# First attention of a two-layer Flamingo block: softmax weights turned by VectorE blocks and SBUF transfers, with scores two batches ahead of values

## The chip, the core and the metric

The kernel runs on one core of one Trainium2 chip. The metric is the device time of one execution in microseconds. The core has five engines that work side by side, each in its own order: TensorE (PE for the matmul, PEld for the load of the stationary operand), VectorE (DVE), ScalarE (ACT), GpSimd (POOL) and SyncE (SP), which here issues transfers. They wait for one another through semaphores. Matrix products land in PSUM, in tiles of 128 partitions × 512 float32 values[...]. Everything is float32.

## The reference, cut to what matters

The inputs are `x` of 16 batches × 128 tokens × 512 and a latent context `ctx` of 16 × 128 × 128. Two layers follow each other, each an attention and a feed-forward part, each added to `x` through a tanh gate. Only the first attention is changed:

```python
q_hk  = (layernorm(x) @ Wq.T).reshape(b, s, 16, 128)
q_big = einsum('bshk,hkq->bshq', q_hk, w_kc_q)
kv    = rope(ctx)                                   # b, l, 128
q_r   = einsum('bshq,hqr->bhsr', q_big, W_qr)       # r = 64
k_r   = einsum('bld,hdr->bhlr', kv, W_kr)
attn  = softmax(einsum('bhsr,bhlr->bhsl', q_r, k_r))
ctx_c = einsum('bhsl,bld->bhsd', attn, kv)
out   = einsum('bhsd,hkd->bshk', ctx_c, w_kc_kv).reshape(b, s, 2048) @ Wo.T
x     = x + tanh(g) * out
```

After it come a mixture-of-experts part with low-rank updates (f0), a causal attention with 16 heads of 32 (a1) and a feed-forward part of eight low-rank experts (f1).

## The kernel before, in words

**Stages.** The profiled execution has five stages: folding of weights until 97.9 us, first attention until 597.3, f0 until 1334, a1 until 1641, f1 until the end at 1860. The batches stand in four groups (`NG`) of four (`GB`); the 16 heads stand in eight pairs (`NPAIR`).

**Folds.** The three query projections of a head are multiplied into one matrix `fq` while weights load ("inward" fold). As a pair's `fq` is done, the keys (`key`) and queries (`query`) of group 0 for that pair follow. Then the "outward" fold multiplies the value projection of each head into the output projection: for each pair, SP loads `wckv_p` and `wo_p` (four buffers each), TensorE makes `o_ps` (L304), and `evacuate` copies it to `fo`. `evacuate` gives its copies to VectorE (L75) and ScalarE (L77) in turn.

**A group.** For groups 1 to 3 the kernel loads the latents, rotates them on GpSimd (`rope`), transposes them (`kvtr`, L189), normalises and transposes four batches of `x` (`layernorm_T`, `xtr`, L133), and makes eight pairs of `k_ps` (L196) and `q_ps` (L204). This is the long stretch of keys and queries. Then come the four batches. `attend` works on half a batch, that is eight heads: 16 score matmuls (L349) into two PSUM tiles of four heads each, then for each tile `exp_normalised`: the maximum on VectorE (`nmx`, L143), four exponentials on ScalarE (L148), the reciprocal of the sum on VectorE (`rden`, L153), and the multiplication on GpSimd (L155). The result `e` has queries on its partitions.

**Transposes and values.** The product with the latents needs latent positions on the partitions. `gather` therefore transposes each of a tile's four heads on TensorE against the identity (`etr`, L368), copies the tile out (`eT`), multiplies it with the rotated latents (`c_ps`, L372) and copies that out (`c`). After both halves of a batch, sixteen matmuls add the heads up to `y_ps` (L391), and VectorE adds that to `x` (`residual`, L138).

**Order.** The loop makes the scores of the next half batch ahead of `gather` of the present one. Beyond that, a scheduler places instructions by their dependencies, and PSUM buffers decide: four tiles in `ps_mm` (scores, keys, queries, `y_ps`, `o_ps`), two in `ps_tr` (transposes), two in `ps_acc` (`c_ps`).

**Loads for f0.** They stand on SP's queue (L315 to L329) once the outward fold has been issued: `w1` (4 MB), the factors `a1`, `b1`, `a2`, `b2`, and small ones. The load of `w2` waits for the last `y_ps`, since it takes the place of `fo`.

Of the kernel before, what the change touches and what calls it, by code (L numbers as in the profile page):

```python
# [15 lines left out]
P = 128  # L16
NB = 16
# [13 lines left out]
LORA_SCALE = 2.0  # L31
HD = 32
K2 = 8
R2 = 64
EPS = 1e-5
MASKED = -3.4028234663852886e38
# [3 lines left out]
def kernel(  # L40
# [93 lines left out]
            evacuate(xnT[:, :, ts(i, P)], tr.rearrange("p (c t) -> p c t", t=P))  # L134
        return xnT

    def residual(b, ps, gate):
        nc.vector.scalar_tensor_tensor(xt[b], ps, gate, xt[b], ALU.mult, ALU.add)  # L138

# [20 lines left out]
    with tc.tile_pool(name="a0", bufs=2) as ap, tc.tile_pool(name="a0s", bufs=3) as sp:  # L160

        def load_kv(g):
            kv = ap.tile([P, GB, P], F32, tag="kv", name=f"kv_{g}", bufs=1)
            nc.sync.dma_start(
                out=kv, in_=kvc[g * GB : (g + 1) * GB].rearrange("b l d -> l b d")
            )
            return kv

        def rope(g, kv):
            kvr = ap.tile([P, GB, P], F32, tag="kvr", name=f"kvr_{g}", bufs=1)  # L170
            rot = ap.tile([P, GB, P], F32, tag="e", name=f"rot_{g}", bufs=3)
            half = P // 2
            cos_b = cos_sb.unsqueeze(1).to_broadcast([P, GB, P])
            nc.gpsimd.tensor_tensor(kvr, kv, cos_b, ALU.mult)
            for lo, hi in ((0, half), (half, 0)):
                nc.gpsimd.tensor_tensor(
                    rot[:, :, lo : lo + half], kv[:, :, hi : hi + half],
                    sin_sb[:, lo : lo + half].unsqueeze(1).to_broadcast([P, GB, half]),
                    ALU.mult,
                )  # L180
            nc.gpsimd.tensor_tensor(
                kvr[:, :, :half], kvr[:, :, :half], rot[:, :, :half], ALU.subtract
            )
            nc.gpsimd.tensor_tensor(
                kvr[:, :, half:], kvr[:, :, half:], rot[:, :, half:], ALU.add
            )
            tr = tr_tile(f"kvtr_{g}")
            for i in range(GB):
                nc.tensor.transpose(tr[:, ts(i, P)], kvr[:, i, :], ident)  # L189
            kvT = ap.tile([P, GT], F32, tag="kv", name=f"kvT_{g}", bufs=1)  # L190
            evacuate(kvT, tr)
            return kvr, kvT

        def key(g, p, kvT):
            k_ps = mm_tile(f"k_ps{g}_{p}")
            nc.tensor.matmul(k_ps, wkr_sb[:, ts(p, P)], kvT, start=True, stop=True)  # L196
            k_p = ap.tile([P, GT], F32, tag=f"k{p}", name=f"k_{g}_{p}", bufs=1)
            evacuate(k_p, k_ps)
            return k_p

        def query(g, p, xnT):
            q_ps = mm_tile(f"q_ps{g}_{p}")
            for c in range(ND):
                nc.tensor.matmul(  # L204
                    q_ps, fq[:, c, ts(p, P)], xnT[:, c, :],
                    start=(c == 0), stop=(c == ND - 1),
                )
# [5 lines left out]

        kvr_0 = kvT_0 = xnT_0 = None
        k_0, q_0 = [], []
        with tc.tile_pool(name="fold", bufs=3, side="right") as fp:
            kv_0 = load_kv(0)
            for b in range(GB):
# [57 lines left out]
            for p in range(1, 3):  # L276
                load_pair(p)
            m_next = fold_first(0)
            kvr_0, kvT_0 = rope(0, kv_0)
            for p in range(NPAIR):  # L280
                m_now = m_next
                if p + 3 < NPAIR:
# [6 lines left out]
                    xnT_0 = layernorm_T("a0", 0)  # L289
                q_0.append(query(0, p, xnT_0))  # L290

            for p in range(NPAIR):
                wckv_p = fp.tile([P, 2, P], F32, tag="wckv", name=f"wckv_{p}", bufs=4)
                nc.sync.dma_start(
                    out=wckv_p, in_=wckv[2 * p : 2 * p + 2].rearrange("h k d -> k h d")
                )
                wo_p = fp.tile([P, 2, D], F32, tag="wo", name=f"wo_{p}", bufs=4)
                nc.sync.dma_start(
                    out=wo_p,
                    in_=woT[2 * p * P : (2 * p + 2) * P, :].rearrange("(h p) d -> p h d", p=P),  # L300
                )
                for j in range(2):
                    o_ps = mm_tile(f"o_ps{p}_{j}")
                    nc.tensor.matmul(  # L304
                        o_ps, wckv_p[:, j, :], wo_p[:, j, :], start=True, stop=True
                    )
                    evacuate(fo[:, 2 * p + j, :], o_ps)

        for b in range(GB, NB):
            nc.scalar.dma_start(out=xt[b], in_=x[b])  # L310


        wf = ctx.enter_context(tc.tile_pool(name="wf", bufs=1, side="right"))
        w1_sb = wf.tile([P, ND, FF], F32, tag="w1_sb", name="w1_sb")
        nc.sync.dma_start(out=w1_sb, in_=f_w1.rearrange("(c p) f -> p c f", p=P))  # L315
        a1_sb = wf.tile([P, ND, E * ER], F32, name="a1_sb")
        nc.sync.dma_start(out=a1_sb, in_=f_a1T.rearrange("(c p) r -> p c r", p=P))
        b1_sb = wf.tile([P, FF], F32, name="b1_sb")
        nc.sync.dma_start(out=b1_sb, in_=f_b1T)
        a2_sb = wf.tile([P, NF, E * ER], F32, name="a2_sb")  # L320
        nc.sync.dma_start(out=a2_sb, in_=f_a2T.rearrange("(c p) r -> p c r", p=P))
        b2_sb = wf.tile([P, D], F32, name="b2_sb")
        nc.sync.dma_start(out=b2_sb, in_=f_b2T)
        nc.sync.dma_start(out=wr_sb, in_=f_wr.rearrange("(c p) e -> p c e", p=P))
        nc.sync.dma_start(out=br_sb, in_=f_br.partition_broadcast(P))
        nc.sync.dma_start(out=bias1_sb, in_=f_b1.rearrange("(c p) -> p c", p=P))
        nc.sync.dma_start(out=bias2_sb, in_=f_b2.partition_broadcast(P))
        nc.sync.dma_start(out=mw2_sb, in_=m_w2.rearrange("(c p) e -> p c e", p=P))
        nc.sync.dma_start(out=mb1_sb, in_=m_b1.rearrange("(c p) -> p c", p=P))  # L329
        nc.sync.dma_start(out=mb2_sb, in_=m_b2.partition_broadcast(P))  # L330

        for g in range(NG):
            if g == 0:
                kvr, k_r, q_r = kvr_0, k_0, q_0
            else:
                kvr, kvT = rope(g, load_kv(g))
                xnT = layernorm_T("a0", g)
                k_r, q_r = [], []
                for p in range(NPAIR):
                    k_r.append(key(g, p, kvT))  # L340
                    q_r.append(query(g, p, xnT))

            def attend(i, hf):
                scores = [mm_tile(f"s_ps{g}_{i}_{hf}_{j}") for j in range(2)]
                for n in range(4):
                    p = 4 * hf + n
                    for j in range(2):
                        rows = slice(j * R, (j + 1) * R)
                        nc.tensor.matmul(  # L349
                            scores[j][:, ts(n, P)],  # L350
                            q_r[p][rows, ts(i, P)], k_r[p][rows, ts(i, P)],
                            start=True, stop=True,
                        )
                es = []
                for j in range(2):
                    n = f"{g}_{i}_{hf}_{j}"
                    e = ap.tile([P, 4 * P], F32, tag="e", name=f"e_{n}", bufs=3)
                    exp_normalised(sp, scores[j], e, f"a0_{n}")
                    es.append(e)
                return es  # L360

            def gather(i, hf, es):
                cx = []
                for j in range(2):
                    n = f"{g}_{i}_{hf}_{j}"
                    tr = tr_tile(f"etr_{n}")
                    for m in range(4):
                        nc.tensor.transpose(tr[:, ts(m, P)], es[j][:, ts(m, P)], ident)  # L368
                    eT = ap.tile([P, 4 * P], F32, tag="eT", name=f"eT_{n}")
                    evacuate(eT, tr)  # L370
                    c_ps = acc_tile(f"c_ps{n}")
                    nc.tensor.matmul(c_ps, kvr[:, i, :], eT, start=True, stop=True)  # L372
                    c_sb = ap.tile(
                        [P, 4 * P], F32, tag=f"c{hf}{j}", name=f"c_{n}", bufs=1
                    )
                    evacuate(c_sb, c_ps)
                    cx.append(c_sb)
                return cx

            steps = [(i, hf) for i in range(GB) for hf in range(2)]  # L380
            ahead, cx = attend(*steps[0]), {}
            for s, (i, hf) in enumerate(steps):
                now = ahead
                if s + 1 < len(steps):
                    ahead = attend(*steps[s + 1])
                cx[hf] = gather(i, hf, now)
                if hf == 0:
                    continue
                o_ps = mm_tile(f"y_ps{g}_{i}")
                for h in range(H):  # L390
                    nc.tensor.matmul(  # L391
                        o_ps, cx[h // 8][h % 2][:, ts(h % 8 // 2, P)], fo[:, h, :],
                        start=(h == 0), stop=(h == H - 1),
                    )
                residual(g * GB + i, o_ps, gate_x[0])

    w2_sb = wp.tile([P, NF, D], F32, tag="w32a", name="w2_sb")
    for s in range(2):
# [401 lines left out]
```

## Time and profile before

| what | value |
|---|---|
| median of 3 runs | 1858.1 us (1855.93 to 1862.87) |
| profiled execution, its own time | 1862.03 us |
| its span | 1860.2 us |
| TensorE busy in the span | 1792.7 us, 96% |
| first attention, 97.9 to 597.3 us | 499.4 us |
| its batches (four stretches) | 102.2 + 98.3 + 103.5 + 93.1 us |
| its keys and queries (three stretches) | 34.3 + 33.7 + 34.3 us |

A row of the profile names the line, the engine, the operation, the output and the inputs, the shapes and the count, then the busy time in us and the mean time of one in ns, then the engine's idle time just before these instructions with what ended it. The mean of a matmul is that of one instruction from its start to its modelled end. Matmuls overlap, so what a sequence of them takes is read from the chain of waits or from the timeline, where a run of equal instructions has a start and a length. "x28" counts passes: a float32 matmul with 512 columns is recorded as two.

### The profile page before, as it was taken

The numbers are of one execution on the slowest core, as the hardware profiler recorded it, in microseconds if no ns is written. First come the engines' busy times: TensorE is split into PE (matmuls) and PEld (weight loads), VectorE is DVE, ScalarE is ACT, GpSimd is POOL, SyncE is SP. The second block draws the span as 40 slices with busy tenths as digits, with TensorE's granted clock in tenths as the row PEclk, the third lists the DMA queues.
The fourth block names the chain that finished last, engine by engine and source line by source line (L and its number), as shares of the span: only waits on it lengthen the run. The fifth ranks groups of instructions, "written<-read, shape, count | busy, mean of one in ns | idle before, by whom it ended". The sixth has DMA issues, their size and how long they took to land.

```text
span 1860.2 us, 16590 instructions
## 1 busy us (share of the span) xinstructions
PE 1792.7 (96%) x6240; PEld 905.7 (49%) x6240; DVE 631.2 (34%) x1228; ACT 504.2 (27%) x1526; POOL 245.6 (13%) x249
## 2 busy tenths in 40 slices
PE   6999999999999999999999999999899999999998
PEld 5554454444445444444444444444465655654444
DVE  4232222322322442143224322442254555622221
ACT  2242142232332321032103210321053644611100
POOL 1022022022011111011101110111020311300000
PEclk9999999999999999999999999999979789799999
DMA  9340000000101100000000000001000000000000
GB/s 324 95 156 1 5 3 0 6 1 1 57 1 40 51 1 0 0 0 1 0 0 1 0 0 0 1 0 68 11 1 6 7 1 1 1 0 23 23 23 23
DMA packets 31328, 43.45 MB, mean 23 GB/s; under 512 B 5776, under 2 KB 16784, under 8 KB 30608
## 3 DMA queue, kind: packets, MB, share of 16 engines
q1 hardware_dynamic: 28224, 37.54, 5.9%
q10 hardware_dynamic: 3024, 4.85, 0.7%
q8 instruction: 49, 0.80, 0.2%
q14 instruction: 31, 0.25, 0.0%
HBM read 38.20 MB, written 4.19 MB: 23 GB/s over the span
## 4 chain that ended last, share of the span: by engine, by line
PE 91%; DVE 3%; DMA 2%; ACT 2%; POOL 1%; issue 1%; ACTq 0%; SPq 0%; DVEq 0%; POOLq 0%
PE fy_ps L552 12%; PE y_ps L391 12%; PE h_ps L506 12%; PE t_ps L532 6%; PE l_ps L517 6%; PE q_ps L204 6%; PE vx_ps L707 3%; PE my_ps L724 3%; PE y_ps L656 3%; PE c_ps L372 3%; PE h_ps L675 3%; PE q_ps L597 3%; PE s_ps L615 2%; PE e1tr L639 2%; PE o_ps L647 2%; PE k_ps L196 1%
## 5 line engine op out<-in xcount | busy, mean ns | idle before, releaser
L506 PE MATMUL h_ps<-xnT_f,w_sb 128*128 128x512 f32 x512 | 240.6, 592 | 0.0
L391 PE MATMUL y_ps<-fo,c 128*128 128x512 f32 x512 | 227.0, 594 | 1.6 <-DVE c L75 1.6
L155 POOL TENSOR_TENSOR e<-e,rden_a 128x512 f32<-128x512 f32 x128 | 132.7, 1039 | 714.1 <-DVE rden_a L153 581.6
L552 PE MATMUL fy_ps<-w_sb,mix 128*128 128x512 f32 x512 | 223.0, 592 | 0.0
L521 DVE TENSOR_TENSOR a<-l_ps,base 128x512 f32<-128x512 f32 x128 | 88.5, 692 | 248.7 <-PE l_ps L517 248.3
L552 PEld LDWEIGHTS fy_ps<-w_sb,mix 128*128 128x128 f32 x512 | 97.3, 190 | 122.4 <-issue 121.5
L506 PEld LDWEIGHTS h_ps<-xnT_f,w_sb 128*128 128x128 f32 x512 | 97.0, 190 | 120.5 <-issue 120.5
L391 PEld LDWEIGHTS y_ps<-fo,c 128*128 128x128 f32 x512 | 95.4, 190 | 114.7 <-issue 111.0
L526 POOL TENSOR_TENSOR mix<-a,a 128x512 f32<-128x512 f32 x64 | 80.9, 1264 | 366.6 <-DVE a L523 366.6
L517 PE MATMUL l_ps<-t,b_sb 128*128 128x512 f32 x256 | 121.4, 594 | 0.2 <-DVE t L495 0.2
L532 PE MATMUL t_ps<-a,a_sb 128*128 128x512 f32 x256 | 120.5, 593 | 0.1
L204 PE MATMUL q_ps<-xnT_a,fq 128*128 128x512 f32 x256 | 115.5, 594 | 3.3 <-ACT xnT_a L77 2.0
L148 ACT ACTIVATE e<-s_ps,nmx_a 128x128 f32<-128x128 f32 x256 | 90.2, 394 | 89.8 <-DVE nmx_a L143 82.3
L511 ACT ACTIVATE base<-h_ps,bias_sb 128x512 f32<-128x512 f32 x64 | 44.0, 687 | 225.3 <-PE h_ps L506 225.3
L148 ACT ACTIVATE e<-e,nmx_a 128x128 f32<-128x128 f32 x256 | 98.9, 390 | 13.2 <-DVE nmx_a L143 13.2
L522 ACT ACTIVATE a<-a 128x512 f32<-128x512 f32 x128 | 80.6, 630 | 73.6 <-DVE a L521 73.5
L138 DVE SCALAR_TENSOR_TENSOR x<-y_ps,gates,x 128x512 f32<-128x512 f32 x32 | 24.0, 750 | 225.1 <-PE y_ps L391 191.6
L523 DVE TENSOR_TENSOR a<-a,wT 128x512 f32<-128x512 f32 x128 | 87.8, 686 | 6.3
L560 DVE SCALAR_TENSOR_TENSOR fy<-bias_sb,wsum,fy_ps 128x512 f32<-128x512 f32 x16 | 12.0, 747 | 205.4 <-PE fy_ps L556 205.4
L204 PEld LDWEIGHTS q_ps<-xnT_a,fq 128*128 128x128 f32 x256 | 48.4, 190 | 63.8 <-issue 57.7
L517 PEld LDWEIGHTS l_ps<-t,b_sb 128*128 128x128 f32 x256 | 48.0, 190 | 58.8 <-issue 57.4
L532 PEld LDWEIGHTS t_ps<-a,a_sb 128*128 128x128 f32 x256 | 42.9, 188 | 67.5 <-DVE a L523 63.6
(153 smaller groups left out, 2125.9 us busy)
## 6 DMA issues: line engine op xcount, KB each, us to landing
x<-in_x ACTq DMA_DIRECT2D x16, 256.0 KB, 6.1
wq<-in_wq SPq DMA_DIRECT2D x8, 512.0 KB, 5.7
wo<-in_woT SPq DMA_DIRECT2D x8, 512.0 KB, 5.9
w_sb<-in_f_w SPq DMA_DIRECT2D x1, 4096.0 KB, 12.6
w_sb<-in_f_w SPq DMA_DIRECT2D x2, 2048.0 KB, 12.1
out<-x SPq DMA_DIRECT2D x16, 256.0 KB, 2.0
wcq<-in_wcqT SPq DMA_DIRECT2D x8, 384.0 KB, 6.2
kv<-in_kvc SPq DMA_DIRECT2D x8, 256.0 KB, 2.8
```

The lines of the kernel that those rows point to most:

```text
L148: nc.scalar.activation(dst[:, ts(i, P)], src[:, ts(i, P)], AF.Exp, bias=nmx[:, i : i + 1], accum_out=den[:, i : i + 1],)
L155: nc.gpsimd.tensor_tensor(d3, d3, rden.unsqueeze(2).to_broadcast([P, 4, P]), ALU.mult)
L204: nc.tensor.matmul(q_ps, fq[:, c, ts(p, P)], xnT[:, c, :], start=(c == 0), stop=(c == ND - 1),)
L391: nc.tensor.matmul(o_ps, cx[h // 8][h % 2][:, ts(h % 8 // 2, P)], fo[:, h, :], start=(h == 0), stop=(h == H - 1),)
L506: nc.tensor.matmul(h_ps, w1_sb[:, c, ts(f, P)], xnT[:, c, :], start=(c == 0), stop=(c == ND - 1),)
L517: nc.tensor.matmul(l_ps, b1_sb[:, ts(f, P)], t1[k], start=True, stop=True)
L521: nc.vector.tensor_tensor(a, l_ps, base, ALU.add)
L522: nc.scalar.activation(a, a, AF.Gelu_apprx_tanh)
L523: nc.vector.tensor_tensor(a, a, wT[k], ALU.mult)
L526: nc.gpsimd.tensor_tensor(m, act[0], act[1], ALU.add)
L532: nc.tensor.matmul(t2_ps[k], a2_sb[:, f, :], act[k], start=(f == 0), stop=(f == NF - 1),)
L552: nc.tensor.matmul(y_ps, mix[f][:, ts(i, P)], w2_sb[:, f, :], start=(f == 0), stop=False,)
```

## The change

It does the following in the first attention.

1. The `etr` transposes on TensorE and the `eT` copies go. VectorE transposes each tile of `e` in blocks of 32 × 32 in place (`nc.vector.transpose`, into `eb`), and 16 transfers a batch on SP's queue carry the blocks to their partitions: block row `q`, block column `k` of all 16 heads at once, from `eb` to `eT` (`carry`).
2. Scores are made by whole batches, into all four `ps_mm` tiles, and two batches ahead (`AHEAD`): step `s` does `gather(s - 2)`, `score(s)`, `project(s - 2)`, `carry(s)`. The transposes of the next group's latents and normalised rows stand between `score` and `project` in steps 2 and 3 of a group, the keys and queries after `project` in step 3.
3. The scores of batches 0 and 1 stand ahead of the outward fold. Its first four loads are issued ahead of the small f0 loads, the others as the folds go, and `carry(0)` after the last of them.
4. TensorE's instructions and SP's transfers of this stage keep the order in which they are written (`keep_in_program_order`).
5. `k_ps`, `q_ps`, `c_ps` and `o_ps` move to the two `ps_tr` tiles; `y_ps`, `kvtr` and `xtr` share the two `ps_acc` tiles. `kvr` gets two buffers, and `kvT` one of its own.
6. The loads of `a1`, `w1` (now in quarters), `b1`, `a2` and `b2` are issued in the last step, after `gather(15)` and ahead of `project(15)`.

```diff
+BK = 32
+NK = P // BK
+AHEAD = 2
...
+    def matmul(*args, **kw):
+        ins = nc.tensor.matmul(*args, **kw)
+        if ordered[0]:
+            tc.keep_in_program_order(ins)
...
+    def send(dst, src):
+        ins = nc.sync.dma_start(out=dst, in_=src)
+        if ordered[0]:
+            tc.keep_in_program_order(ins)
...
+        def score(b):
+            g, i = divmod(b, GB)
+            scores = [mm_tile(f"s_ps{b}_{t}") for t in range(4)]
...
+            eb = rp.tile([P, H, P], F32, tag="eb", name=f"eb_{b}")
+            eTs[b] = rp.tile([P, H, P], F32, tag="eT", name=f"eT_{b}")
+            for t in range(4):
+                e = ap.tile([P, 4 * P], F32, tag="e", name=f"e_{b}_{t}", bufs=3)
+                exp_normalised(sp, scores[t], e, f"a0_{b}_{t}")
+                nc.vector.transpose(
+                    eb[:, 4 * t : 4 * t + 4, :], e.rearrange("p (n l) -> p n l", l=P)
+                )
...
+        def carry(b):
+            for q in range(NK):
+                for k in range(NK):
+                    send(eTs[b][ts(k, BK), :, ts(q, BK)], ebs[b][ts(q, BK), :, ts(k, BK)])
+
+        def gather(b):
+            g, i = divmod(b, GB)
+            cxs[b] = []
+            for t in range(4):
+                c_ps = tr_tile(f"c_ps{b}_{t}")
+                matmul(
+                    c_ps, roped[g][0][:, i, :],
+                    eTs[b][:, 4 * t : 4 * t + 4, :].rearrange("p n q -> p (n q)"),
+                    start=True, stop=True,
+                )
+                c_sb = ap.tile([P, 4 * P], F32, tag=f"c{t}", name=f"c_{b}_{t}", bufs=1)
+                evacuate(c_sb, c_ps)
+                cxs[b].append(c_sb)
...
+        ordered[0] = True
+        for s in range(AHEAD):
+            score(s)
+        for p in range(NPAIR):
+            fold_outward(p, *outward[p])
+            if p + 4 < NPAIR:
+                outward.append(load_outward(p + 4))
+            if p == 3:
+                carry(0)
+        for s in range(NB + AHEAD):
+            b = s - AHEAD
+            g = s // GB + 1
+            if b >= 0:
+                gather(b)
+            if AHEAD <= s < NB:
+                score(s)
+            if s == NB + AHEAD - 1:
...
+                send(a1_sb, f_a1T.rearrange("(c p) r -> p c r", p=P))
...
+            if g < NG and s % GB == 2:
+                latents(g)
+            if g < NG and s % GB >= 2:
+                for i in range(2):
+                    normalise(g, s % GB * 2 - 4 + i)
+            if b >= 0:
+                project(b)
+            if 0 < s < NB:
+                carry(s)
+            if g < NG:
+                if s % GB == 0:
+                    kv_next = load_kv(g)
+                elif s % GB == 1:
+                    roped[g] = rope(g, kv_next)
+                    deviations(g)
+                elif s % GB == 3:
+                    k_r[g], q_r[g] = [], []
+                    keys_and_queries(g, range(NPAIR))
+        ordered[0] = False
-            def gather(i, hf, es):
-                cx = []
-                for j in range(2):
-                    n = f"{g}_{i}_{hf}_{j}"
-                    tr = tr_tile(f"etr_{n}")
-                    for m in range(4):
-                        nc.tensor.transpose(tr[:, ts(m, P)], es[j][:, ts(m, P)], ident)
-                    eT = ap.tile([P, 4 * P], F32, tag="eT", name=f"eT_{n}")
-                    evacuate(eT, tr)
...
```

## The prediction

> **What bounds the kernel now.** The page comes first, for the engine that limits:
>
> ```profile
> PE 1792.7 (96%) x6240; PEld 905.7 (49%) x6240; DVE 631.2 (34%) x1228; ACT 504.2 (27%) x1526; POOL 245.6 (13%) x249
> ```
>
> TensorE is busy 96% of the span; VectorE has two thirds of its time free, ScalarE nearly three quarters. The change touches the first attention alone, 97.9 to 597.3 us, so I next cut that stage at its own seams (the key and query stretches of groups 1 to 3 are the second, fourth and sixth piece) and take each engine's busy time from the table of windows:
>
> ```profile
> 97.90:200.10 102.20, 96.49 (x375) 49.74 (x374) 30.34 (x59) 33.76 (x149) 20.69 (x21) 0.97 0.18 67
> 200.10:234.40 34.30, 34.30 (x88) 15.36 (x90) 8.43 (x18) 6.16 (x10) 0.00 (x0) 1.00 0.03 8
> 234.40:332.70 98.30, 93.52 (x369) 48.17 (x367) 29.58 (x62) 35.85 (x150) 20.70 (x21) 0.98 0.00 1
> 366.40:469.90 103.50, 96.53 (x375) 49.84 (x374) 30.29 (x59) 33.96 (x149) 20.69 (x21) 0.97 0.00 1
> 504.20:597.30 93.10, 90.13 (x348) 46.11 (x347) 24.62 (x51) 32.91 (x146) 16.63 (x16) 0.98 0.07 23
> 97.90:597.30 499.40, 478.96 (x1711) 239.36 (x1711) 138.94 (x278) 153.31 (x618) 78.71 (x79) 0.98 0.06 21
> ```
>
> The columns are length, then busy time of PE, PEld, DVE, ACT and POOL, granted clock, DMA share, GB/s. TensorE idles 20.4 us of 499.4, all of it in the four stretches of batches; the DMA engines are all but empty (share 0.06). So time leaves this stage only if TensorE is given less to do or idles less. What it does, by shape:
>
> ```profile
> L391 PE MATMUL y_ps<-fo,c 128*128 128x512 f32 x512 | 227.0, 594 | 1.6 <-DVE c L75 1.6
> L368 PE MATMUL etr<-ident,e 128*128 128x128 f32 x256 | 40.6, 294 | 5.1 <-POOL e L155 4.7
> L75 DVE COPY eT<-etr 128x512 f32<-128x512 f32 x32 | 20.9, 682 | 10.4 <-PE etr L368 10.4
> L77 ACT COPY eT<-etr 128x512 f32<-128x512 f32 x32 | 19.1, 633 | 98.7 <-PE etr L368 98.7
> ```
>
> The transposes of the weights are the only TensorE work that the change removes; their copies out cost engines that have room. Last, the order at the stage's start:
>
> ```profile
> 97.84 2.06 PE L349 MATMUL s_ps<-k,q 64*128 64x128 f32 x32
> 101.31 1.16 PE L349 MATMUL s_ps<-k,q 64*128 64x128 f32 x8 [1.42 <-ACT e L148]
> ...
> 105.97 3.78 PE L372 MATMUL c_ps<-eT,kvr 128*128 128x512 f32 x4
> ```
>
> **The change part by part.** A batch now costs, by chained rows: y_ps 12.02 us for 28 passes, 0.429 each, so 32 make 13.74; c_ps eight passes, 3.43; scores 32 in 2.0 (the 2.06 above).
>
> *Transposes removed.* Eight take 1.04 to 1.34 us in sequence (not their 294 ns each: they overlap), so 16 take 2.3 to 2.6 us, 256 some 37 to 41 by either reckoning, and part of the 5.1 us idle before them goes too. The 64 copies that leave (VectorE 20.9, ScalarE 19.1 us) free time that nobody waits for.
>
> *VectorE's transposes added.* Four a batch, 128x512; no row shows the operation. Below: the 539 ns of a normalisation between SBUF tiles; above: twice the 682 ns copy. I take the copy. Four make 2.8 us a batch in place of 1.4 us of copies, on an engine with some 70% free: nothing on the path, 0 to +3 us a batch of delay to the transfers.
>
> *Transfers added.* 256 on SP's queue, 16 a batch, each 512 pieces of 128 bytes (64 KB): 512 pieces for each of 16 DMA engines a batch. They wait for the batch's fourth transpose, and c_ps two steps later waits for the last of them. Issue is 16 × 0.47, some 7.5 us a batch. For the pieces, the nearest row is a latent load, 512 pieces of 512 bytes, alone on the queues:
>
> ```profile
> 1336.00:1336.50 0.50, 0.00 (x0) 0.00 (x0) 0.00 (x0) 0.00 (x0) 0.00 (x0) 0.50 0.11 31
> 1336.50:1337.00 0.50, 0.00 (x0) 0.00 (x0) 0.00 (x0) 0.00 (x0) 0.00 (x0) 0.50 0.36 108
> 1337.00:1337.50 0.50, 0.00 (x0) 0.00 (x0) 0.00 (x0) 0.00 (x0) 0.00 (x0) 0.50 1.01 304
> 1337.50:1338.00 0.50, 0.00 (x0) 0.00 (x0) 0.00 (x0) 0.00 (x0) 0.00 (x0) 0.50 0.28 82
> ```
>
> Shares 0.11 + 0.36 + 1.01 + 0.28 of 0.5 us on 16 engines are 14.1 engine-us, 27.5 ns a piece. At the same 27.5 ns for 128 bytes a batch occupies the queues 14.1 us[...]. From above, a bias load of 2048 four-byte pieces held SP's next issue 3.50 us, 128 pieces an engine, at most 27 ns each. I take 14 us and keep 7 to 30. The window is wide: from the end of a batch's scores, weights are ready after about 7.5 us and read after two steps less the scores, 33 us, so 26 us; and in the long run a batch may take a step, 19.7 us (38 ns a piece). By this the transfers are hidden.
>
> [...] The row speaks for overlap: 256 KB moved in about 2 us with issue at 0.4 us spacing[...]. I go by the row[...].
>
> *Scores two batches ahead, order kept.* Gather waits vanish if transfers are in time, but TensorE, now strictly in order, picks up others: where the next group's latents and normalised rows are transposed (three times), the two-buffer PSUM pool waits for a copy on ScalarE queued behind all four tiles' exponentials. Scores' first tile is ready at 0.5 us, maximum 0.69, sixteen exponentials at 0.344 make 5.5, copy 0.59: 7.3 us after the scores began, against 2.0 of scores and about 1 of transposes, a wait of 4.3; 4.9 in the middle group, where VectorE's queue adds 0.6. The following step waits about 0.9 for a normalised copy. Sum 13.5 + 2.7 = 16 us. TensorE pauses then bring the second price:
>
> ```profile
> 104.00:110.00 6.00, 5.92 (x15) 3.11 (x15) 1.92 (x5) 3.91 (x19) 2.08 (x2) 0.50 0.99 413
> ```
>
> After a 1.4 us pause the granted clock is 0.50 for some 6.4 us (c_ps above took 3.78 us instead of 1.7): 3.3 us lost. [...] I take 10.5. (Before lost about 10 in the same way.)
>
> *Outward folds behind the first scores.* Scores of batch 0 start near 82.5 instead of 97.8; those of batch 1 wait for tiles to be read, to about 91. The 16 folds are 13.7 us of passes, but their evacuations queue behind exponentials and transposes, and pairs 4 to 7 load only as buffers come free; end about 112. SP queues batch 0's transfers behind the last pair's issue; they leave from about 105 to 115 and land near 118, so gather(0) starts at 118 where it started at 106. That costs 12 us, against two batches of scores already done (4.0) and folds that no longer follow.
>
> *Moved loads.* The MoE weights are asked for after gather(15) instead of at 98 us. SP holds nothing else then; y_ps(15) covers 13.7 us, and w1's first quarter (1 MB, about 3 us at the 413 GB/s above) is needed some 13 us after the stage's end: nothing, at worst +10. The next latents' loads and rotation start a step or more before their use: nothing.
>
> **Sum.** From 118: sixteen steps of 3.43 + 2.0 + 13.74 + 0.5 of small waits = 19.7, 315.2, less 4.0 of scores done, 311.2; three key and query stretches at 34.3, 102.9; 60 transposes for them at 0.145, 8.7; waits 16; clock 10.5. The stage ends at 567.3, against 597.3: 30 us less on the profiled span of 1860.2 (own time 1862.0, within the runs shown: 1855.9 to 1862.9). From the median of 1858.1: **1828 us**.
>
> **The rivals.**
> *Cheaper pauses.* If the copies interleave better or a pause brings no half clock, 10 to 18 us of the last two terms stay away: about 1814. For it: VectorE shares the evacuations. Against: the order on each engine is fixed.
> *Transfers somewhat late.* At 24 us a batch they fit the mean (a group has 79 + 37 us for 96) but not four steps in a row: two steps a group late by about 2.4 and 4.3 us, 27 us over four groups, of which 10 fall into waits already counted: about 1845.
> *Transfers as the bound (slower).* The place is c_ps waiting for SP's queue. With X us a batch the stage ends near 122 + 16X, even with before at X = 29.7: 58 ns a piece, 1.86 us a transfer. At 64 ns X is 32.8, the end 647, the time 1908; at 75 ns some 1991. For it: no run shows 128-byte pieces between SBUF tiles, each piece from 32 partitions only[...]. Against: 27 ns at most in both rows.
> That TensorE is not relieved cannot be: 256 of its instructions are gone.
>
> **How the numbers follow.** Forecast 0.58, cheaper pauses 0.16, somewhat late 0.13, transfers as the bound 0.13. A difference under 0.5%, 9.3 us, cannot be told from none in this kernel. Faster takes the first two and half of the third: 0.80; same the other half and a little: 0.07; slower 0.13. The range, 1805 to 1866, takes in the first three with the unknown prices (start ±8, waits −16 to +10, moved loads to +10) and leaves out the fourth and a tail below.
>
> **What would show it.** Right: no etr row, c_ps without long waits for DMA, stage end near 567, batch steps near 20 us, three clock dips of some 6 us a group apart. Wrong: SP's transfers 1.5 us or more apart and c_ps idle behind them; score matmuls waiting on exponentials in every step; h_ps waiting for w1; gather(0) far from 118.

## Result and the profile after

The changed kernel takes 1836.5 us, median of four runs (1834.9 to 1839.3), beside 1860.5 for the kernel before (1855.9 to 1863.0): a ratio of 0.9875, 95% interval 0.9849 to 0.9901, or 24 us less. Forecast were 30 us less and 1828, with 1805 to 1866 as the range. The profiled execution has a span of 1833.1 us, 27.1 below that of before; the other 3 us are the place of the two profiled executions among their runs.

The rows by shape of the changed kernel, from 80 to 620 us; the columns are those of before:

```profile
L144 PE MATMUL y_ps<-fo,c 128*128 128x512 f32 x512 | 230.8, 610 | 5.4 <-DVE xnT_a L78 3.2 <-ACT kvT L80 2.1
L144 PE MATMUL c_ps<-eT,kvr 128*128 128x512 f32 x128 | 63.7, 634 | 8.2 <-DMA eT<-eb 7.3 <-DVE c L78 0.9
L401 DVE STREAM_TRANSPOSE eb<-e 128x512 f32<-128x512 f32 x64 | 45.5, 710 | 58.5 <-POOL e L176 57.4 <-DMA eT<-eb 1.1
L144 PEld LDWEIGHTS q_ps<-xnT_a,fq 128*128 128x128 f32 x192 | 34.7, 189 | 50.2 <-issue 35.9 <-ACT q L80 9.0 <-DVE q L78 5.3
L149 PE MATMUL xtr_a<-ident,xn_a 128*128 128x128 f32 x48 | 8.0, 304 | 9.5 <-DVE xnT_a L78 6.3 <-DVE kvT L78 3.2
```

The `etr` row is gone. In its place VectorE has 64 block transposes of 0.71 us, close to the copy that the forecast took. Of all values only the first waited for a transfer (7.3 us). What the other steps wait for stands at `xtr_a` and `y_ps`: copies on VectorE and ScalarE. The page's list of transfers adds their time to landing:

```profile
eT<-eb SPq DMA_DIRECT2D x256, 64.0 KB, 2.3
```

The windows of the stage, cut at its own seams (length, busy PE, PEld, DVE, ACT, POOL, granted clock, DMA share, GB/s):

```profile
80.40:118.50 38.10, 25.12 (x97) 11.90 (x96) 17.22 (x33) 16.32 (x72) 8.31 (x8) 0.81 0.46 98
118.50:171.40 52.90, 47.74 (x165) 23.37 (x166) 20.86 (x43) 18.05 (x74) 12.45 (x13) 0.88 0.34 51
171.40:206.30 34.90, 34.90 (x81) 14.60 (x80) 6.88 (x10) 4.10 (x7) 0.00 (x0) 1.00 0.13 20
206.30:294.50 88.20, 83.11 (x308) 39.94 (x308) 37.14 (x74) 31.90 (x142) 20.72 (x21) 0.96 0.28 43
294.50:330.40 35.90, 35.90 (x82) 14.81 (x81) 6.29 (x9) 4.69 (x8) 0.00 (x0) 1.00 0.14 20
330.40:420.00 89.60, 84.03 (x309) 40.10 (x308) 37.17 (x74) 31.80 (x142) 20.73 (x21) 0.96 0.28 43
420.00:455.00 35.00, 35.00 (x82) 14.69 (x81) 6.88 (x10) 4.10 (x7) 0.00 (x0) 1.00 0.18 35
455.00:567.90 112.90, 112.90 (x370) 52.01 (x369) 34.78 (x66) 30.43 (x141) 16.62 (x16) 1.00 0.43 99
```

The stage ends at 567.9 us (forecast 567.3). The last window is the change as it was meant: TensorE is busy throughout at full clock, although transfers fill 43% of the DMA engines' time (the loads for f0 at its end among them). What is left of pauses and half clock in this stage lies in the rows with a clock below 1.00: the start, and the end of each of the first three groups. TensorE's timeline there:

```profile
118.55 6.53 PE L144 MATMUL c_ps<-eT,kvr 128*128 128x512 f32 x8 [7.27 <-DMA eT<-eb]
125.01 2.06 PE L144 MATMUL s_ps<-k,q 64*128 64x128 f32 x32
127.00 0.66 PE L149 MATMUL kvtr<-ident,kvr 128*128 128x128 f32 x4
127.49 0.60 PE L149 MATMUL xtr_a<-ident,xn_a 128*128 128x128 f32 x4
131.26 1.11 PE L149 MATMUL xtr_a<-ident,xn_a 128*128 128x128 f32 x4 [3.17 <-DVE xnT_a L78]
133.22 16.34 PE L144 MATMUL y_ps<-fo,c 128*128 128x512 f32 x32 [0.84 <-ACT kvT L80]
```

Two waits of 3.17 and 0.84 us stand between scores and outputs. The copies that end them:

```profile
129.86 0.71 DVE L401 STREAM_TRANSPOSE eb<-e 128x512 f32<-128x512 f32 x1 [0.56 <-POOL e L176]
130.55 0.66 DVE L78 COPY xnT_a<-xtr_a 128x512 f32<-128x512 f32 x1
132.49 0.68 ACT L80 COPY kvT<-kvtr 128x512 f32<-128x512 f32 x1
```

The long wait ends with VectorE's copy, which stands behind the block transpose of the new batch's first tile, and that behind GpSimd's multiplication. The short one ends with ScalarE's copy, behind the exponentials of all four tiles. The outputs then take 16.34 us where this view has 14.00 in an undisturbed step. The granted clock in one-microsecond windows says why:

```profile
136.00:137.00 1.00, 1.00 (x3) 0.48 (x2) 0.94 (x3) 0.00 (x0) 0.03 (x1) 0.50 0.00 0
137.00:138.00 1.00, 1.00 (x3) 0.47 (x2) 0.60 (x3) 0.30 (x1) 0.00 (x0) 0.52 0.00 0
138.00:139.00 1.00, 1.00 (x3) 0.38 (x2) 0.17 (x1) 0.00 (x0) 0.00 (x0) 1.00 0.75 107
```

From 132 to 138 us it is one half (the last column but two).

### The profile page after: what moved, and what is told of

Read it like the earlier page. It is cut to its first block, busy times and chain, and to the rows that moved or that the text cites. A ratio compares the mean times of both kernels' runs of the same rounds, so it can differ in the third digit from the quotient of the medians.

```text
span 1833.1 us, 16301 instructions
## 1 busy us (share of the span) xinstructions
PE 1758.6 (96%) x5984; PEld 870.6 (47%) x5984; DVE 653.8 (36%) x1260; ACT 488.6 (27%) x1494; POOL 245.7 (13%) x249
## 4 chain that ended last, share of the span: by engine, by line
PE 88%; DVE 4%; DMA 2%; SPq 2%; ACT 2%; POOL 1%; issue 1%; ACTq 0%; POOLq 0%; DVEq 0%
PE fy_ps L652 12%; PE h_ps L606 12%; PE y_ps L144 11%; PE q_ps L144 6%; PE t_ps L632 6%; PE l_ps L617 6%; PE vx_ps L807 3%; PE my_ps L824 3%; PE y_ps L756 3%; PE h_ps L775 3%; PE q_ps L697 3%; PE c_ps L144 3%; PE s_ps L715 2%; PE e1tr L739 2%; SPq L154 2%; PE o_ps L747 2%
## 5 line engine op out<-in xcount | busy, mean ns | idle before, releaser
L144 PE MATMUL y_ps<-fo,c 128*128 128x512 f32 x512 | 230.8, 610 | 5.4 <-DVE xnT_a L78 3.2
L176 POOL TENSOR_TENSOR e<-e,rden_a 128x512 f32<-128x512 f32 x128 | 133.2, 1043 | 696.6 <-DVE rden_a L174 648.0
L144 PE MATMUL q_ps<-xnT_a,fq 128*128 128x512 f32 x256 | 118.5, 606 | 3.5 <-DVE mv_a L354 3.5
## 6 DMA issues: line engine op xcount, KB each, us to landing
w_sb<-in_f_w SPq DMA_DIRECT2D x4, 1024.0 KB, 10.7
```

Of the source, the lines that this page charges most:

```text
L144: ins = nc.tensor.matmul(*args, **kw)
L176: nc.gpsimd.tensor_tensor(d3, d3, rden.unsqueeze(2).to_broadcast([P, 4, P]), ALU.mult)
```

## Experiments

The theory: the gain is TensorE's transposes, which now lie beside its other work because two steps of lookahead cover the transfers; part of it is paid back at the start and at three waits with their half clock. The rivals: the lookahead and the fixed order gain by themselves; or the transfers are near the point where they set the pace. All times are medians; the changed kernel's is 1836.5, and before was 1860.1 to 1861.1 beside each of these.

### Transposes back on TensorE, in the new order

```diff
-                e = ap.tile([P, 4 * P], F32, tag="e", name=f"e_{b}_{t}", bufs=3)
+                e = eb[:, 4 * t : 4 * t + 4, :].rearrange("p n l -> p (n l)")
                 exp_normalised(sp, scores[t], e, f"a0_{b}_{t}")
-                nc.vector.transpose(
-                    eb[:, 4 * t : 4 * t + 4, :], e.rearrange("p (n l) -> p n l", l=P)
-                )
...
-                    send(eTs[b][ts(k, BK), :, ts(q, BK)], ebs[b][ts(q, BK), :, ts(k, BK)])
+            for t in range(4):
+                tr = tr_tile(f"etr_{b}_{t}")
+                for m in range(4):
+                    transpose(tr[:, ts(m, P)], ebs[b][:, 4 * t + m, :], ident)
+                evacuate(
+                    eTs[b][:, 4 * t : 4 * t + 4, :],
+                    tr.rearrange("p (n q) -> p n q", q=P),
+                )
```

> The changed kernel's order and lookahead, with the weights transposed on TensorE again, in the place where the transfers were issued. Theory (the gain is the TensorE work that went to VectorE and the queues): 16 x (2.3 to 2.6) = 37 to 42 us come back, less some 7 us since the first values no longer wait for transfers; 1865 to 1880 us, slower than the kernel before. Rival (the gain is the lookahead of two batches and the fixed order): at most 1850.

Measured: 1867.3 us, a ratio to before of 1.0040 (1.0024 to 1.0055). The rival falls: order, lookahead and the moved folds by themselves make the kernel some 7 us slower, and moving the transposes off TensorE is worth 31. Its TensorE timeline shows the work that came back:

```profile
249.40 1.04 PE L149 MATMUL etr<-ident,eb 128*128 128x128 f32 x8
251.09 1.06 PE L149 MATMUL etr<-ident,eb 128*128 128x128 f32 x8 [0.66 <-DVE eT L78]
252.50 3.89 PE L144 MATMUL c_ps<-eT,kvr 128*128 128x512 f32 x8 [0.34 <-DVE eT L78]
```

From one batch's values to the next this step takes 22.75 us (229.75 to 252.50), where the changed kernel's takes 19.54: 2.1 us of transposes and 1.0 of waits for their copies.

### One step of lookahead

```diff
-AHEAD = 2
+AHEAD = 1
```

> AHEAD = 1 in place of 2. Theory (the transfers are hidden by the second batch of lookahead): in the changed kernel a batch's last transfer lands 24.4 us after its scores begin (229.4 to 253.8); with one step between, values are due after 15.9, so TensorE waits 8.5 us in some 12 steps, about 100 us, and each such wait brings 2 to 3 us of half clock: 1935 to 1970. Rival (the transfers are short enough for one step): within 20 us of 1836.

Measured: 1928.9 us, 92 more than the changed kernel; a little less than expected, and far from the rival. Its waits:

```profile
PE c_ps L144 <- DMA eT<-eb: 86.4, 12, 9.9
```

Twelve waits for transfers, 7.2 us each. So the transfers are not short; the second batch of lookahead hides them.

### Transposes for the next group ahead of the scores

```diff
+            if g < NG and s % GB == 2:
+                latents(g)
+                normalise(g, 0)
+            if g < NG and s % GB == 3:
+                normalise(g, 2)
+                normalise(g, 3)
             if AHEAD <= s < NB:
                 score(s)
...
             if g < NG and s % GB == 2:
-                latents(g)
-            if g < NG and s % GB >= 2:
-                for i in range(2):
-                    normalise(g, s % GB * 2 - 4 + i)
+                normalise(g, 1)
```

> The transposes of the next group's latents and rows put ahead of the scores of steps 2 and 3 (the second row's behind), so that their copies stand ahead of the exponentials. Theory: the waits there (12.4 us in the three steps 2, 3.3 in the three steps 3) and the half clock behind them (2.6 + 2.1 + 3.1) go, 23 us: 1812 to 1820. Rival (the pause only moves, to the PSUM tile or to the values' copies): 1830 to 1840.

Measured: 1808.8 us, a ratio of 0.9728 (0.9709 to 0.9747): 27.7 us less than the changed kernel, more than was expected. The same place in its timeline has no wait, and the outputs follow at once at full clock:

```profile
125.19 0.60 PE L149 MATMUL kvtr<-ident,kvr 128*128 128x128 f32 x4
125.62 0.60 PE L149 MATMUL xtr_a<-ident,xn_a 128*128 128x128 f32 x4
126.15 2.06 PE L144 MATMUL s_ps<-k,q 64*128 64x128 f32 x32
128.14 0.66 PE L149 MATMUL xtr_a<-ident,xn_a 128*128 128x128 f32 x4
128.63 13.90 PE L144 MATMUL y_ps<-fo,c 128*128 128x512 f32 x32
```

So the waits were a matter of order on ScalarE and VectorE: a copy behind the new scores' exponentials and block transposes is late, the same copy ahead of them is not. The stage ends 24.9 us earlier (its last outputs end at 543.0). Of the remaining 2.8 us, 1.9 lie behind the stage (1263.3 us to the end of the span instead of 1265.2) and 0.9 between the runs.

### The first transfers ahead of the late outward loads

```diff
+        carry(0)
-        for p in range(NPAIR):
+        for p in range(4):
             fold_outward(p, *outward[p])
-            if p + 4 < NPAIR:
-                outward.append(load_outward(p + 4))
-            if p == 3:
-                carry(0)
+            outward.append(load_outward(p + 4))
...
+            if s == AHEAD:
+                for p in range(4, NPAIR):
+                    fold_outward(p, *outward[p])
             if AHEAD <= s < NB:
                 score(s)
```

> The first batch's transfers issued ahead of the outward loads of pairs 4 to 7, and those pairs folded after the first values. Theory (the start costs what it does because the transfers stand behind the last loads): first values at 105 to 107 instead of 118.5, the later folds end by 117, so everything after is 8 to 12 us earlier: 1824 to 1829. Rival (the late loads of pairs 4 to 7 take the place of that wait): 1834 or more.

Measured: 1828.6 us, 8 less, as the theory has it. The first values start at 108.5 instead of 118.5 us, although this execution came out of the inward folds 3.2 us later.

### Twice and three times as many transfers

```diff
-                    send(eTs[b][ts(k, BK), :, ts(q, BK)], ebs[b][ts(q, BK), :, ts(k, BK)])
+                    for lo, hi in zip(cuts, cuts[1:]):
+                        send(
+                            eTs[b][ts(k, BK), :, q * BK + lo : q * BK + hi],
+                            ebs[b][ts(q, BK), :, k * BK + lo : k * BK + hi],
+                        )
```

with `cuts` of (0, 16, 32) and of (0, 10, 20, 32); the bytes stay the same.

> Each transfer cut into two of half the columns: 32 a batch, 512 pieces of 64 bytes each, the same bytes. Theory (SP's issue, 0.67 us each, sets the pace and a batch may take a step): 21.4 us a batch, ready 35 us after its scores begin where 39 are to be had; late by a few us at the end of a group, about 12 us at the start: 1842 to 1856. Rival (the pieces set the pace, or landing times grow with the number under way): 1865 or more.

> Each transfer cut into three (10, 10 and 12 columns): 48 a batch. Theory: 32 us a batch, above the 29.7 from which the transfers were said to outweigh the gain: the last batch lands near 104 + 16 x 32 + 2 = 618, its values and outputs end near 637, 69 us later than in the changed kernel: about 1905, slower than before. Rival (much of the transfers' time is covered even so): at most 1870.

Measured: 1855.0 us with halves (ratio to before 0.9967, 0.9953 to 0.9980) and 1950.8 with thirds (1.0484, 1.0459 to 1.0510). Halves are at the edge of what was expected. Their profiled execution is 21.6 us longer than that of the changed kernel; it came out of the inward folds 3.3 us later, and loses 9.2 more at the start (first outputs at 145.7 instead of 133.2). Thirds are 46 us beyond the theory, so its sum lacks something. SP's own waits in the run with thirds:

```profile
SPq L154 <- DVE eb L401: 23.7, 3, 9.0
SPq L154 <- PE c_ps L144: 6.4, 1, 6.4
```

SP starves, three times, 9.0, 8.4 and 6.4 us, once at each of the later groups. The first scores of a group stand behind the long stretch of keys and queries. When that stretch ends late, because its group's values waited for transfers, SP has sent all it had and waits for the new weights. The queue and TensorE then hold each other up in turn. These waits and another 6.4 us for a buffer that `c_ps` still read make 30 of the 46 us; the rest was not traced.

### Outward folds first

```diff
-        for s in range(AHEAD):
-            score(s)
         for p in range(NPAIR):
             fold_outward(p, *outward[p])
             if p + 4 < NPAIR:
                 outward.append(load_outward(p + 4))
-            if p == 3:
-                carry(0)
+        for s in range(AHEAD):
+            score(s)
+        carry(0)
```

> The outward folds ahead of the first scores, as in the kernel before; everything else as in the changed kernel. Theory: folds end at 95 to 98, the first batch's weights are ready near 110, its transfers land near 123, so the first values start 4 to 5 us later than at 118.5: 1840 to 1842. Rival (the fixed order made the folds slow, and folding first gives that back): 1834 or less.

Measured: 1838.5 us (1836.6 to 1839.4), too near 1836.5 to part from it. The first values start at 122.4, 3.8 us later, as expected. But they then take 5.66 us instead of 6.53, and the first outputs 15.70 instead of 16.34, so the stage ends 1.8 us later. Here the 32 passes of folds take 15.8 us almost without a break (81.3 to 97.1). In the changed kernel they take 21 (90.1 to 111.3), behind others' copies and in part at half clock (until 93.59, and from 97.00 to 100.41). The time lies between the two sides of the expectation: placing scores first gains almost nothing as it stands.

### Both edits, and what stood between them

> The two edits together: transposes for the next group ahead of scores, and the first transfers ahead of the late outward loads. Theory (the two terms are apart from one another): the sum of both gains, 31 to 35 us: 1801 to 1806. Rival (they share a cover): under 25 us, above 1811.

Measured: 1813.8 us (ratio 0.9748, 0.9731 to 0.9764). The gains did not add up, and the time lies where the rival was put; it is no better than with the one edit alone (1808.8, ratio 0.9728). The cause is another wait, not a shared cover. In this kernel the transposes for group 1 stood ahead of the late folds:

```profile
105.72 3.87 PE L144 MATMUL c_ps<-eT,kvr 128*128 128x512 f32 x8 [1.87 <-DMA eT<-eb]
119.94 1.12 PE L149 MATMUL kvtr<-ident,kvr 128*128 128x128 f32 x4 [10.36 <-POOL kvr L203]
```

The values came early, and TensorE then stood for 10.36 us at a transpose whose operand GpSimd had not rotated: the latents' load stood on SP behind the first transfers and the loads of pairs 4 to 7. The mend is to load them first and to put the folds ahead of the transposes (shown against the kernel with both edits):

```diff
+        kv_next = load_kv(1)
         carry(0)
...
+            if s == AHEAD:
+                for p in range(4, NPAIR):
+                    fold_outward(p, *outward[p])
             if g < NG and s % GB == 2:
                 latents(g)
                 normalise(g, 0)
...
-            if s == AHEAD:
-                for p in range(4, NPAIR):
-                    fold_outward(p, *outward[p])
...
-                    kv_next = load_kv(g)
+                    if g > 1:
+                        kv_next = load_kv(g)
```

> The two edits together once more, with what went wrong in e8_both mended: the latents of group 1 are loaded ahead of the first transfers, and the outward folds of pairs 4 to 7 stand ahead of the transposes for group 1 instead of behind them. Theory (in e8_both TensorE waited 10.36 us at kvtr for the rotation on GpSimd, whose load stood behind the transfers): first outputs start at 120 to 122 instead of 128.6 in e3_turns_first, 5 to 8 us less than it. Rival (the start is bound by the folds' copies and the half clock, not by this wait): no difference from e3_turns_first over 2 us.

> e3_turns_first unchanged, beside e9_latents_early on the same chip: 1807 to 1811.

Measured: 1802.5 us (ratio 0.9685, 0.9666 to 0.9704), beside 1810.4 for the single edit on the same chip (0.9730, 0.9712 to 0.9747). This is the fastest version, 58 us below the kernel before and 34 below the changed one.

```profile
108.77 3.98 PE L144 MATMUL c_ps<-eT,kvr 128*128 128x512 f32 x8
112.59 7.80 PE L144 MATMUL o_ps<-wo,wckv 128*128 128x512 f32 x16
120.23 0.60 PE L149 MATMUL kvtr<-ident,kvr 128*128 128x128 f32 x4
120.66 0.60 PE L149 MATMUL xtr_a<-ident,xn_a 128*128 128x128 f32 x4
121.19 2.06 PE L144 MATMUL s_ps<-k,q 64*128 64x128 f32 x32
```

The first values wait for nothing, the late folds run in one piece, and `kvtr` finds its operand ready. The first outputs start at 123.7 us, 5 earlier than with the single edit (128.6), though not at the 120 to 122 that were expected.

## Why the prediction was right, and where it was not

**The mechanism held.** Transposes leave TensorE and nothing takes their place in a steady step: 19.54 us against 19.7 forecast, hidden behind two batches of lookahead as the forecast had it. The transposes were put at 37 to 41 us. With them back in the new order each step is 3.2 us longer, 51 in sum, since their copies are waited for as well. The stage's end moves by 35 (567.9 to 603.1): that kernel starts its values 2.9 us sooner, has two batches' transposes done by then (6.4) and runs the first values at nearly full clock (2.6). These make 47 of the 51.

**The start.** Gather(0) was put at 118 us and began at 118.55, for the reason given: SP's queue behind the last outward load. The values themselves then ran at half clock (0.50 until 124.31), 6.53 us instead of 3.79: a fourth dip beside the three that were forecast.

**The waits.** Forecast were 4.3, 4.9 and 4.3 us; they are 4.01, 3.98 and 4.47. ScalarE's copy ends within 0.1 us of each pause's end, as forecast; that VectorE's copy holds TensorE for the first 3.17 us of it was not named, and the extra 0.6 us of the middle group did not appear. The waits of the following step, 0.9 each by forecast, are 1.1 in all three groups. The half clock was put at 10.5 for three dips. These cost 2.3, 1.8 and 2.8 us in the outputs, 7.0 in sum; the fourth, 2.7, brings the sum to 9.7. That this is near 10.5 is luck. That the waits of the three groups and their dips were a price is shown by the edit that removes them and gains 27.7.

**Not foreseen.** The key and query stretches take 34.9, 35.7 and 34.9 us by the chain of waits, 2.6 more in sum than the 34.3 each that was carried over. The change gives `k_ps` and `q_ps` two PSUM tiles instead of four, and TensorE's loads now wait for ScalarE's and VectorE's `q` copies (9.0 and 5.3 us in the `q_ps` row above). In the kernel before they waited for no such copy:

```profile
L204 PEld LDWEIGHTS q_ps<-xnT_a,fq 128*128 128x128 f32 x192 | 36.2, 190 | 47.8 <-issue 45.9 <-ACT xnT_a L77 1.8
```

The change names the move of tiles; the forecast gave it no price. No run moves these tiles alone, so the cause is read from the rows and not tried. The stage's end was met within 0.6 us, in part by luck: sixteen steps came out 2.6 us shorter and the three dips 3.5 cheaper, against 2.6 for the stretches and 2.7 for the fourth dip.

Behind the stage, the time to the end of the span is 1265.2 us instead of 1262.9. The moved loads account for at most 0.4 of this: the runs with transposes on TensorE and with transposes ahead of the scores load in the same place, and take 1263.2 and 1263.3. From the first `r_ps` to the first `h_ps` it is 13.1 us in the changed kernel and 11.9 in before and in these two. Just behind the stage's end its clock is one half for 10.2 us (571.45 to 581.69), that of before for 6.8 (602.11 to 608.93). This places 1.2 of the 2.3 us; the rest stays open.

So 30 us became 24 by 0.6 at the stage's end, 2.3 behind it, and 3.2 because the profiled executions stand above the median before and below it after. The kernel before, at 1860.5 beside it instead of 1858.1, makes the other 2.4 us of the way from 1828 to 1836.5.

**Transfers: sound verdict, wrong terms.** The forecast took 27.5 ns for a piece and 0.47 us for an issue. Over one batch's transfers the window is

```profile
241.00:254.00 13.00, 11.01 (x59) 5.78 (x57) 5.01 (x9) 4.26 (x20) 4.22 (x6) 1.00 0.57 83
```

0.57 of 13 us on each engine is 7.4 us for 512 pieces: 14.5 ns each, half of what was taken; the 7.4 us are near the 7 that the forecast kept, by estimate, as its lower end. SP's issue is 0.63 us, 0.67 from one to the next, so a batch's 16 occupy the queue 10.7 us. It is the issue (10.7 us) and not the pieces (7.4) that sets a batch's time, and both err within the window of 26 us. The row of the forecast spoke for overlap, and so it came out: a transfer takes 2.3 us to land, and the next is issued 0.67 us after the one before.

**The slower rival's point was too far away.** It was put at 29.7 us a batch. Halves, 32 × 0.67 = 21.5 us, already give back 18.5 of the 24 us; thirds, 32 us, lose 114. A straight line between the two, an estimate, crosses the time of before near 22 us. The sum "122 + 16 X" spread each group's slack evenly over its batches. It left out that the start is lengthened too and that SP starves behind the key and query stretch. At 10.7 us the changed kernel has twice the room, not nearly three times. One sum of this rival has a slip: at 75 ns a piece it gives 1997 us, not 1991.

## What to carry to other kernels

A transpose can leave a saturated TensorE (96% busy before) for a VectorE with room (34%) and idle queues (a DMA share of 0.06) if its result is needed more than a full chain later: here 24.4 us from scores to the last landing, hidden by two batches of lookahead and not by one, which left twelve waits of 7.2 us. When TensorE's order is fixed by hand, look at what stands ahead of each copy on the engines that empty its PSUM tiles: moving three groups of transposes ahead of the scores gained more than the whole change (27.7 us beside 24). And where two edits each gain, follow the next operand of what has become early; it may be the one that nobody needed so soon.

## What the hardware showed beyond expectation

In these runs small pieces between SBUF tiles stop getting cheaper at about 10 ns. At 128 bytes a piece takes 14.5 ns of a DMA engine. A window of the run with halves holds 32 transfers, 1024 pieces for each engine:

```profile
233.30:255.00 21.70, 21.70 (x79) 10.26 (x78) 7.81 (x15) 6.86 (x34) 4.16 (x4) 1.00 0.47 46
```

0.47 of 21.7 us is 10.0 ns a piece of 64 bytes. One of the run with thirds holds 70, 2240 pieces each:

```profile
224.70:280.70 56.00, 47.69 (x164) 21.71 (x162) 17.00 (x32) 15.40 (x71) 8.32 (x8) 0.97 0.41 28
```

0.41 of 56 us is 10.2 ns a piece of 40 to 48 bytes. The issue on SP did not follow the bytes: 0.67 us for 512 pieces whether of 128, 64 or 40 bytes.

In the profiled execution of the changed kernel the times at which the granted clock changes lie whole multiples of one interval apart. In windows of 0.1 us it falls at

```profile
131.10:131.20 0.10, 0.00 (x0) 0.00 (x0) 0.10 (x1) 0.10 (x3) 0.10 (x1) 0.66 0.00 0
254.00:254.10 0.10, 0.00 (x0) 0.00 (x0) 0.10 (x1) 0.10 (x3) 0.00 (x0) 0.56 0.00 0
380.30:380.40 0.10, 0.00 (x0) 0.00 (x0) 0.10 (x1) 0.10 (x3) 0.00 (x0) 0.53 0.00 0
```

A mean of 0.66 is full clock for a third of the window and one half for the rest, so the first fall is at 131.13; the others are at 254.01 and 380.31. Read in this way, the twelve falls and rises between 80 and 420 us (86.76, 93.59, 97.00, 100.41, 114.06, 124.31, 131.13, 137.96, 254.01, 260.84, 380.31, 387.13) all lie whole multiples of 3.413 us apart (within 0.02). So three equal pauses of 3.17 us, which began at 128.09, 252.01 and 376.27, brought the fall 3.0, 2.0 and 4.0 us after TensorE stopped: twice within the pause, once behind it. Each of the three dips lasts twice 3.413, 6.8 us; so does the one behind the pause of 1.4 us in the kernel before (103.76 to 110.59).

The length of a pause alone does not decide whether the clock falls. In the run with the first transfers early TensorE stood for 1.85 us until 100.20 and for 1.73 us until 108.48, and the clock fell only behind the first:

```profile
100.20 6.55 PE L144 MATMUL o_ps<-wo,wckv 128*128 128x512 f32 x10 [1.85 <-DVE fo L78]
108.48 3.87 PE L144 MATMUL c_ps<-eT,kvr 128*128 128x512 f32 x8 [1.73 <-DMA eT<-eb]
```

```profile
100.00:101.00 1.00, 0.80 (x2) 0.49 (x3) 0.22 (x2) 0.30 (x1) 0.63 (x1) 1.00 0.73 108
101.00:102.00 1.00, 1.00 (x3) 0.27 (x1) 0.56 (x1) 0.00 (x0) 0.41 (x1) 0.61 0.70 99
102.00:103.00 1.00, 1.00 (x3) 0.16 (x1) 0.79 (x3) 0.00 (x0) 0.64 (x1) 0.50 0.63 87
...
108.00:109.00 1.00, 0.52 (x2) 0.31 (x3) 0.00 (x0) 0.00 (x0) 0.00 (x0) 1.00 1.07 162
109.00:110.00 1.00, 1.00 (x4) 0.36 (x2) 0.00 (x0) 0.39 (x1) 0.00 (x0) 1.00 0.74 285
```

The half clock behind the first lasts from 101.22 to 104.64. Behind the second the clock is full, and the values take 3.87 us, where those at half clock in the changed kernel took 6.53. In the kernel before, a pause of 1.42 us was followed by half clock; here one of 1.73 us was not. What else decides it is not shown here.
